# Fifteen of sixteen DMA engines for a weight load on the software queue, in place of fourteen

## The chip, the core and the metric

The kernel runs on one core of a Trainium2 chip. The metric is the device time in microseconds of one execution. A single profiled execution gives the durations below; the time before is the median of three other runs.

## The reference, cut to what matters

```python
# r_inputs [1024, 32, 128] float32, W [496, 128, 128] float32
I_IDX, J_IDX = the 496 pairs i < j of the 32 fields
transformed = einsum('bpd,ped->bpe', r_inputs[:, I_IDX, :], W)
y = transformed * r_inputs[:, J_IDX, :]          # [1024, 496, 128] float32, 260 MB
```

For each pair (i, j) of fields, field i is multiplied by the pair's own 128x128 matrix, and the product elementwise by field j. The matrices are 32.5 MB, the result 260 MB.

## The kernel before

The host lays the inputs out by field, transposed: a field is a tile of 128 partitions by 1024 columns (the batch). Pairs run from the last field backwards (`_pairs`), and each pair `q` has two halves of 512 columns. The first 15 pairs are multiplied in float32 directly (L267). For the other 481, weights and fields are split into a high part, a low part and a correction (`split_w`, L146 to L158; `split_x`, L163 to L177), and a half is three matmuls: two at L270 in `first`, a scaling of the PSUM tile on ScalarE at L272, and one at L281 in `second`, three halves later. VectorE multiplies the finished pair by field j into an output tile (`write`, L246), and ScalarE's queue stores the tile (L321): four pairs a store at first, three from pair 292 on (`FOURS`). Output tiles are a ring of 12 slots, and for a time the memory of fields that are loaded only later.

The program order is written out by hand in the loop at L302. What each step of it does to the DMA queues matters here:

- Stores go over ScalarE's queue, 128 rows each, so each of the 16 DMA engines carries eight rows of each store.
- Fields, and weights of chunks `c` that aren't in `WAPART`, are loaded over SyncE's queue (`load_x`, `load_group`, `load_w`), again eight rows to an engine. A chunk is the weights of eight pairs: a tile of 128 rows of 4 KB. Three tiles take turns (`WB`), and a chunk is loaded when the tile of an earlier one is spent (L327 to L335).
- The 25 chunks in `WAPART` (even `c` from 12 to 60) are loaded by `load_apart` (L113): the first `8 n` rows by one DMA of GpSimd, the software queue, whose source is arranged so that it falls into `n` shares of eight rows, one to an engine; the remaining rows by a DMA of SyncE, one or two to each engine. `n` is 14 for 17 of them and 12 for the other eight (every third, L35).
- The software queue hands its shares to consecutive engines, from where the last DMA ended. `move_on(k)` (L109) is a tiny DMA of `k` shares of two 64-byte rows into a scratch tile; it moves that place by `k`. `START` puts it at engine 5 once (L310). Each load of `n` shares is followed, three pairs later (`BACK`, L315 to L317), by `move_on(16 - n)`, which brings it round to 5. So a load of 14 shares is on engines 5 to 15, 0, 1 and 2, and skips 3 and 4; one of 12 shares skips 1 to 4. Engines are numbered here from the queue's first place.

Of the kernel before, what the change touches and what calls it, by code (L numbers as in the profile page):

```python
# [31 lines left out]

XG = 4
START = 5
WAPART = {c: 12 if k % 3 == 1 else 14 for k, c in enumerate(range(12, 62, 2))}  # L35
WLAST = max(WAPART)
BACK = 3
FOURS = 73
# [19 lines left out]
def kernel(  # L58
# [22 lines left out]
    nc = tc.nc  # L81
# [12 lines left out]
    def load_x(f, pieces=1, eng=None):  # L94
        if f == 0:

            t = rpool.tile([P, WL, P], F32, tag="w", name="x_0").rearrange("p q e -> p (q e)")
        else:
            t = xpool.tile([P, BT], F32, tag=f"x{f}", name=f"x_{f}")
        s = BT // pieces  # L100
        for k in range(pieces):
            (eng or nc.sync).dma_start(out=t[:, k * s : (k + 1) * s], in_=xt[f, :, k * s : (k + 1) * s])
        x_sb[f] = t

    w_raw = {}
# [3 lines left out]
    def move_on(k):  # L109

        nc.gpsimd.dma_start(out=mark[: 2 * k], in_=xt[0, : 2 * k, :16].rearrange("(b a) n -> a b n", a=k))

    def load_apart(c):  # L113
        n = WAPART[c]
        r = 8 * n
        nc.gpsimd.dma_start(out=w_raw[c][:r], in_=wt[c, :r].rearrange("(b a) m n -> a b m n", a=n))
        nc.sync.dma_start(out=w_raw[c][r:], in_=wt[c, r:])

    group = {}

    def load_group(k, m):
        if m == XG - 1:
            group[k] = xpool.tile([P, XG, BT], F32, tag=f"g{k}", name=f"x_g{k}")
        f = XG * k + 1 + m
        x_sb[f] = group[k][:, m, :]
        nc.sync.dma_start(out=x_sb[f], in_=xt[f])

    def load_w(c, splits=(0, WL), eng=nc.sync):
        w_raw[c] = rpool.tile([P, WL, P], F32, tag="w", name=f"w_{c}")
        if c in WAPART:  # L130
            load_apart(c)
            return
        for a, b in zip(splits, splits[1:]):
            eng.dma_start(out=w_raw[c][:, a:b, :], in_=wt[c, :, a:b, :])
# [78 lines left out]
    back = {}  # L213
# [45 lines left out]
    def first(u):  # L259
        q, h = divmod(u, 2)  # L260
        i, c = pairs[q][0], q // WC
        r = slice(q % WC * P, (q % WC + 1) * P)
        s = slice(h * HB, (h + 1) * HB)
        if h == 0:
            po[q] = po_t[q % PB]
        if q < nq0:
            nc.tensor.matmul(po[q][:, s], w_raw[q // WL][:, q % WL, :], x_sb[i][:, s], start=True, stop=True)  # L267
        else:
            for t in (0, 1):
                m = nc.tensor.matmul(po[q][:, s], w_s[c][t][:, r], x_s[i][t][:, s], start=t == 0, stop=t == 1)  # L270
                apart(m, scaled.get(u - 1) if h else None)
            scaled[u] = nc.scalar.mul(po[q][:, s], po[q][:, s], 1.0 + EPS)  # L272
            apart(scaled[u], taken.get(q - PB), "TensorE's products, which this waits for, have waited for it")

    def second(u):
        q, h = divmod(u, 2)
        i, j = pairs[q]
        r = slice(q % WC * P, (q % WC + 1) * P)
        s = slice(h * HB, (h + 1) * HB)
        if q >= nq0:  # L280
            m = nc.tensor.matmul(  # L281
                po[q][:, s], w_s[q // WC][2][:, r], x_s[i][2][:, s], start=False, stop=True, skip_group_check=True
            )
            apart(m, scaled[u ^ 1])
        g, k = group_of[q]
        if k == 0 and h == 0:
            ots[g] = out_tile(g)
        if q >= NQ - 2:
            write(g, k, s, po[q][:, s], x_sb[j][:, s])
        elif h == 1:  # L290
            taken[q] = write(g, k, slice(0, BT), po.pop(q), x_sb[j])
        ot = ots[g][0]
        n = groups[g][1]
        if q >= NQ - 2:
            stores.append((u + SLAG, rows(g)[:, k, s], ot[:, k, s]))
        elif g in (0, len(groups) - 1):
            if h == 1:
                stores.append((u + SLAG, rows(g)[:, k], ot[:, k]))
        elif k == n - 1 and h == 1:
            stores.append((u + SLAG, rows(g), ot))  # L300

    for u in range(2 * NQ + LAG + SLAG):  # L302
        q = u // 2
        if u < 2 * NQ:
            i, j = pairs[q]
            if u % 2 == 0 and j == i + 1 and XG * ngroup < i - 2 - XLEAD:
                load_x(i - 2 - XLEAD)
            first(u)
            if u == 2 * nq0:
                move_on(START)  # L310
            if u % 2 == 0 and q in group_at:
                load_group(*group_at[q])
            if u % 2 == 1 and q in w_at:
                load_w(w_at[q])
            if u % 2 == 0 and q in back:  # L315
                c = back.pop(q)
                move_on(16 - WAPART[c] if c < WLAST else 32 - START - WAPART[c])  # L317
        if LAG <= u < 2 * NQ + LAG:
            second(u - LAG)
        while stores and stores[0][0] <= u - LAG:  # L320
            nc.scalar.dma_start(*stores.pop(0)[1:])  # L321
        if u % 2 == 1:
            ready = [t for t in todo if t[0] <= q]
            if ready:
                ready[0][2](u)
                todo.remove(ready[0])
        if ring[WB:] and ring[0] in spent:  # L327
            ring.pop(0)
            c = ring[WB - 1]
            if c == "x":  # L330
                load_x(0)
            else:
                load_w(c)
            if c in WAPART:
                back[q + BACK] = c  # L335
        while later and later[0][0] <= u:
            nc.vector.tensor_tensor(*later.pop(0)[1:], ALU.subtract)  # L337
# [32 lines left out]
```

## Time and profile before

| | |
|---|---|
| median of three runs | 747.86 us (742.39 to 754.28) |
| the profiled execution's own time | 740.79 us |
| its span, first to last instruction | 738.9 us |
| HBM read, written | 49.29 MB, 260.05 MB; 419 GB/s over the span |
| mean granted TensorE clock | 0.990 |
| issue of a software-queue weight load | 17 of 448 KB, 8 of 384 KB; 0.62 us of GpSimd each |

The span is what the profile covers; the execution's own time is 1.9 us longer. The busy share of an engine is an average over stages; which engine sets the pace is read from the waits. A DMA's time to landing runs from its issue to the last of its 16 completion counts, so it holds the time in which the 16 engines work off what was queued before. The DMA share of a stretch is the time of all packets over 16 times its length.

### The profile page before, as it was taken

How to read it: one execution, taken by the hardware profiler on the slowest of the kernel's cores; microseconds unless marked ns; L12 is line 12 of the kernel's file. 1: busy time of each engine (PE TensorE's matmuls, PEld its weight loads, DVE VectorE, ACT ScalarE, POOL GpSimd, SP SyncE). 2: the span in 40 equal slices, each digit the busy share in tenths (PEclk: the TensorE clock that was granted, in tenths of full speed). 3: DMA queues.
4: the chain of work that ended last, by engine and by line, in shares of the span. 5: the costliest groups of instructions: out<-in, count | busy, mean ns of one | idle time of the engine just before them, and what ended most of it. 6: DMA issues, size and time to landing. Idle time of an engine off the chain costs nothing.

```text
span 738.9 us, 10346 instructions
## 1 busy us (share of the span) xinstructions
PE 702.5 (95%) x2946; PEld 548.9 (74%) x2946; DVE 636.5 (86%) x550; ACT 634.2 (86%) x1256; POOL 596.4 (81%) x882
## 2 busy tenths in 40 slices
PE   7999999999999999999899979999999999999993
PEld 3577777777878888787688858876887777877882
DVE  3888999999999998997789868977998888998894
ACT  1288989999999999998899969988999999998992
POOL 1789999999999999888879867987798878896660
PEclk9999999999999999999999989999999999999997
DMA  9999999999999999999999999999999999999998
GB/s 347 418 430 428 428 427 429 427 423 426 427 419 425 424 421 424 422 424 425 425 425 424 424 425 417 418 420 422 420 425 422 420 423 420 424 417 424 422 430 339
DMA packets 37096, 310.02 MB, mean 420 GB/s; under 512 B 5680, under 2 KB 5808, under 8 KB 19248
## 3 DMA queue, kind: packets, MB, share of 16 engines
q10 hardware_dynamic: 21888, 261.11, 83.8%
q1 hardware_dynamic: 10720, 37.30, 12.5%
q0 software_dynamic: 4432, 10.96, 3.8%
q8 instruction: 24, 0.39, 0.2%
q14 instruction: 32, 0.26, 0.1%
HBM read 49.29 MB, written 260.05 MB: 419 GB/s over the span
## 4 chain that ended last, share of the span: by engine, by line
PE 65%; DMA 19%; DVE 7%; POOL 3%; issue 2%; ACT 2%; SPq 0%; ACTq 0%; POOLq 0%; DVEq 0%
PE po L270 42%; PE po L281 20%; DMA out_dram<-slots 18%; DVE slots L246 4%; PE po L267 3%; DVE xd L337 2%; ACT po L272 2%; POOL wd L155 1%; POOL wl L153 1%; DMA x<-in_xt_dram 1%; POOL xl L170 1%; DVE ot L246 1%; POOL xl L171 0%; POOL wd L154 0%; ACT wh L151 0%
## 5 line engine op out<-in xcount | busy, mean ns | idle before, releaser
L272 ACT ACTIVATE po<-po 128x512 f32<-128x512 f32 x962 | 553.3, 584 | 72.5 <-PE po L270 55.1
L270 PE MATMUL po<-xh,wh 128*128 128x512 f32 x962 | 381.8, 397 | 16.8 <-DVE slots L246 13.5
L281 PE MATMUL po<-xd,wd 128*128 128x512 f32 x962 | 375.8, 391 | 4.8 <-DVE xd L337 2.4
L270 PE MATMUL po<-xl,wl 128*128 128x512 f32 x962 | 376.9, 392 | 1.3 <-POOL wl L153 1.0
L246 DVE TENSOR_TENSOR slots<-po,x 128x1024 f32<-128x1024 f32 (+1 forms) x263 | 313.7, 1213 | 53.0 <-DMA out_dram<-slots 18.7
L270 PEld LDWEIGHTS po<-xh,wh 128*128 128x128 f32 x962 | 181.0, 188 | 74.6 <-DVE slots L246 30.8
L153 POOL TENSOR_TENSOR wl<-w,wh 128x256 fp32r<-128x256 f32 x241 | 185.6, 770 | 61.7 <-ACT wh L151 55.6
L281 PEld LDWEIGHTS po<-xd,wd 128*128 128x128 f32 x962 | 180.9, 188 | 45.0 <-DVE slots L246 3.2
L270 PEld LDWEIGHTS po<-xl,wl 128*128 128x128 f32 x962 | 181.1, 188 | 40.8 <-POOL wl L153 4.0
L155 POOL TENSOR_TENSOR wd<-wl,wd 128x256 fp32r<-128x256 f32 x241 | 182.3, 757 | 20.1
L246 DVE TENSOR_TENSOR slots<-po,x_g 128x1024 f32<-128x1024 f32 x123 | 147.8, 1223 | 25.1 <-DMA out_dram<-slots 12.8
L246 DVE TENSOR_TENSOR ot<-po,x 128x1024 f32<-128x1024 f32 x99 | 119.3, 1221 | 14.0 <-PE po L281 4.9
L154 POOL TENSOR_SCALAR wd<-wh 128x256 fp32r<-128x256 f32 x241 | 102.6, 426 | 20.6
L151 ACT ACTIVATE wh<-w 128x256 fp32r<-128x256 f32 x241 | 98.7, 410 | 5.7 <-DVE slots L246 3.8
L337 DVE TENSOR_TENSOR xd<-xh,xl 128x512 fp32r<-128x512 f32 x52 | 48.1, 925 | 0.0
L170 POOL TENSOR_TENSOR xl<-x_g,xh 128x512 fp32r<-128x512 f32 x32 | 41.7, 1302 | 1.4 <-ACT xh L169 1.1
L170 POOL TENSOR_TENSOR xl<-x,xh 128x512 fp32r<-128x512 f32 x20 | 25.8, 1292 | 15.8 <-ACT xh L169 15.6
L171 POOL TENSOR_SCALAR xl<-xl 128x512 fp32r<-128x512 f32 x52 | 34.2, 658 | 4.6
L267 PE MATMUL po<-x,w 128*128 128x512 f32 x60 | 28.1, 625 | 4.3 <-DMA x<-in_xt_dram 4.3
L267 PEld LDWEIGHTS po<-x,w 128*128 128x128 f32 x60 | 11.6, 198 | 20.0 <-issue 13.7
L169 ACT ACTIVATE xh<-x 128x512 fp32r<-128x512 f32 x20 | 12.3, 624 | 11.5 <-DMA x<-in_xt_dram 11.4
L169 ACT ACTIVATE xh<-x_g 128x512 fp32r<-128x512 f32 x32 | 20.0, 624 | 0.0
(8 smaller groups left out, 49.9 us busy)
## 6 DMA issues: line engine op xcount, KB each, us to landing
out_dram<-slots ACTq DMA_DIRECT2D x67, 1536.0 KB, 12.7
out_dram<-slots ACTq DMA_DIRECT2D x44, 2048.0 KB, 16.4
out_dram<-ot ACTq DMA_DIRECT2D x28, 2048.0 KB, 13.8
w<-in_wt_dram SPq DMA_DIRECT2D x36, 512.0 KB, 10.9
x_g<-in_xt_dram SPq DMA_DIRECT2D x16, 512.0 KB, 16.3
w<-in_wt_dram POOLq DMA_DIRECT2D x17, 448.0 KB, 11.7
x<-in_xt_dram SPq DMA_DIRECT2D x14, 512.0 KB, 9.5
w<-in_wt_dram POOLq DMA_DIRECT2D x8, 384.0 KB, 12.0
```

Source lines behind the costliest of these rows:

```text
L151: halved[c] = nc.scalar.mul(h, raw, 1.0 - 2.0**-13)
L153: nc.gpsimd.tensor_tensor(l, raw, h.bitcast(F32), ALU.subtract)
L154: nc.gpsimd.tensor_scalar(d, h.bitcast(F32), EPS, 1.0, ALU.mult, ALU.mult)
L155: nc.gpsimd.tensor_tensor(d, l.bitcast(F32), d.bitcast(F32), ALU.subtract)
L170: nc.gpsimd.tensor_tensor(l, x_sb[f][:, s], h.bitcast(F32), ALU.subtract)
L171: nc.gpsimd.tensor_scalar(l, l.bitcast(F32), 1.0 / EPS, 1.0, ALU.mult, ALU.mult)
L246: i = nc.vector.tensor_tensor(ot[:, k, s], p, f, ALU.mult)
L267: nc.tensor.matmul(po[q][:, s], w_raw[q // WL][:, q % WL, :], x_sb[i][:, s], start=True, stop=True)
L270: m = nc.tensor.matmul(po[q][:, s], w_s[c][t][:, r], x_s[i][t][:, s], start=t == 0, stop=t == 1)
L272: scaled[u] = nc.scalar.mul(po[q][:, s], po[q][:, s], 1.0 + EPS)
L281: m = nc.tensor.matmul(po[q][:, s], w_s[q // WC][2][:, r], x_s[i][2][:, s], start=False, stop=True, skip_group_check=True)
L337: nc.vector.tensor_tensor(*later.pop(0)[1:], ALU.subtract)
```

## The change

Seventeen of the 25 chunks get `n = 15` in place of 14, so that only engine 4 is skipped; the eight with 12 shares stay as they are. The last eight rows of the seventeen leave SyncE's queue: a second DMA of GpSimd (`rest`) loads them, one row to each of eight consecutive engines, at the place in the program where the place of the queue is brought round. It comes before a `move_on(9)` for chunks with `c % 4 == 2` and behind it for chunks with `c % 4 == 0`, so that the eight rows are on engines 4 to 11 or on 13 to 15 and 0 to 4: 15 + 8 + 9 = 32 shares either way. The last chunk is followed by `move_on(4)`. SyncE issues 17 DMAs less, GpSimd 17 more (887 instructions become 904); the order on the other engines doesn't change.

```diff
-WAPART = {c: 12 if k % 3 == 1 else 14 for k, c in enumerate(range(12, 62, 2))}
+WAPART = {c: 12 if k % 3 == 1 else 15 for k, c in enumerate(range(12, 62, 2))}
...
         nc.gpsimd.dma_start(out=w_raw[c][:r], in_=wt[c, :r].rearrange("(b a) m n -> a b m n", a=n))
-        nc.sync.dma_start(out=w_raw[c][r:], in_=wt[c, r:])
+        if n == 12:
+            nc.sync.dma_start(out=w_raw[c][r:], in_=wt[c, r:])
+
+    def go_round(c):
+
+        def rest():
+            a, b = [t[120:].rearrange("a (b m) n -> a b m n", b=2) for t in (w_raw[c], wt[c])]
+            nc.gpsimd.dma_start(out=a, in_=b)
+
+        if WAPART[c] == 12:
+            move_on(4)
+        elif c == WLAST:
+            rest()
+            move_on(4)
+        elif c % 4:
+            rest()
+            move_on(9)
+        else:
+            move_on(9)
+            rest()
...
-                c = back.pop(q)
-                move_on(16 - WAPART[c] if c < WLAST else 32 - START - WAPART[c])
+                go_round(back.pop(q))
```

## The prediction

> **What bounds the kernel now.** I read the page first (busy shares, slices, DMA queues), then the windows by stage, then the waits, the chain, and the DMA issues.
>
> ```profile
> span 738.9 us, 10346 instructions
> PE 702.5 (95%) x2946; PEld 548.9 (74%) x2946; DVE 636.5 (86%) x550; ACT 634.2 (86%) x1256; POOL 596.4 (81%) x882
> DMA  9999999999999999999999999999999999999998
> q10 hardware_dynamic: 21888, 261.11, 83.8%
> q1 hardware_dynamic: 10720, 37.30, 12.5%
> q0 software_dynamic: 4432, 10.96, 3.8%
> ```
>
> The DMA queues add up to 100.4% of 16 engines' span: q10 (the stores, from ACT) 83.8, q1 (loads from SP) 12.5, q0 (the software queue) 3.8. No DMA engine ever rests.
>
> ```profile
> 20.00:125.00 105.00, 100.76 (x404) 74.73 (x402) 97.02 (x85) 85.12 (x172) 93.31 (x128) 1.00 1.01 428
> 125.00:320.00 195.00, 192.95 (x833) 154.90 (x834) 179.41 (x156) 182.11 (x364) 177.66 (x261) 1.00 1.01 424
> 320.00:690.00 370.00, 355.84 (x1521) 283.22 (x1520) 316.12 (x274) 329.87 (x653) 300.08 (x453) 0.99 1.01 422
> 690.00:735.00 45.00, 37.23 (x161) 29.65 (x159) 35.05 (x31) 33.16 (x65) 21.37 (x34) 0.96 1.00 421
> ```
>
> By stage (stretch, its length, then PE, PEld, DVE, ACT, POOL busy, granted clock, DMA share, GB/s) the DMA share is 1.0 everywhere, and PE is at 96 to 99% until 690 us. Two bounds lie close together; a DMA engine that gets later shows up as a late store:
>
> ```profile
> POOL wl L153 <- ACT wh L151: 55.6, 65, 7.8
> DVE slots L246 <- DMA out_dram<-slots: 31.6, 40, 6.4
> PEld po L270 <- DVE slots L246: 30.8, 44, 5.9
> PEld po L270 <- POOL wl L153: 4.0, 8, 1.2
> PE po L270 <- POOL wl L153: 1.0, 2, 0.8
> ```
>
> (who waits for whom: total us, times, longest). DVE waits 31.6 us for stores to leave their slots, and PE then waits for DVE. PE waits for POOL only 5.0 us in all.
>
> ```profile
> out_dram<-slots ACTq DMA_DIRECT2D x67, 1536.0 KB, 12.7
> w<-in_wt_dram POOLq DMA_DIRECT2D x17, 448.0 KB, 11.7
> w<-in_wt_dram SPq DMA_DIRECT2D x18, 64.0 KB, 6.1
> mark<-in_xt_dram POOLq DMA_DIRECT2D x16, 0.2 KB, 9.5
> L111 POOL DMA_DIRECT2D mark<-in_xt_dram x26: 634/634/748, 31.5 to 679.6; - x26
> L117 SPq DMA_DIRECT2D w<-in_wt_dram x25: 326/326/338, 124.5 to 675.2; - x25
> ```
>
> A store is done when the last of its engines is done, and so is the kernel. The question is therefore which engine is last, and by how much.
>
> **The engines one by one.** A packet in the trace has queue, start, duration and size, and no engine. But each starts 3 or 4 ns before the end of the one ahead of it on its engine, so I strung them, from the end backwards, into 16 chains, each holding its share of every load and store in order. This holds from 331 us on. The software rows name the chains: a 14-share load with the cursor at 5 falls on engines 5 to 15, 0, 1, 2; a 12-share one on 5 to 15 and 0. Last packets end: engines 1 and 2 at 737.5 and 737.0, 0 at 737.0, one of 5 to 15 at 737.3, the others at 734.5 to 735.9; engines 3 and 4, in an order that I can't tell, at 735.6 and 734.0.
>
> Before, the 25 loads give engines 0 and 5 to 15 17x9 + 8x10 = 233 rows each, 1 and 2 169, and 3 and 4 33. So 3 and 4 have 200 rows less, at 155 ns from start to start (a 4 KB packet takes 159) 31 us less work, and still end with the others: their packets are that much slower. Over the medians (611 ns for 16 KB, 460 for 12, 159 for 4) the packets from 345 us on lose: 3 and 4 21.7 and 18.8 us, 1 and 2 7.4 and 8.2, 0 4.2, the other eleven 0.5 to 3.6.
>
> The losses are of two kinds. One of {3, 4} loses 8.8 of its 21.7 us in steps up to 50 ns on nearly every packet, also after 695 us when no load moves: 1.3 us in 700 to 735. Call it the steady one. The other loses 16.7 of its 18.8 us in bursts of 2 to 3 us while a weight load moves, 0.5 to 0.7 us a load; engines 1 and 2 lose in the same bursts. In the bursts, lead matters: 1 and 2 lose 0.6 to 1.2 us in SP loads that find them 0.5 us ahead to 1.3 behind the median, and mostly nothing from 1.8 us behind on. Before 125 us, where no load skips an engine, the stores' landings show one engine drifting behind (3.1 us behind the median at 120 us), a few settling about 1.4 behind, and all packets together lose 1 to 2 us in 20, against 4 to 5 later. So the bursts look like the price of being ahead, and the steady loss belongs to one engine.
>
> **The change, part by part.**
> (1) Rows: in 17 loads 15 shares skip only engine 4, and the last eight rows go one to an engine, nine times to 4 to 11, eight times to 13 to 15 and 0 to 4. Engine 3 has 17x8 + 8 + 16 = 160 rows, +127, or 127 x 0.155 = +19.7 us; engine 4 stays at 33; 0, 1, 2, 13, 14, 15 lose 9 rows (-1.4 us), 5 to 11 8 (-1.2), 12 17 (-2.6).
> (2) Small packets: engine 3 drops 17x8 four-byte dummies (9 ns each, 5 to 6 from start to start), -0.7 us; each new DMA adds about three small ones an engine, 17 x 15 ns = 0.3 us. Together about 0.
> (3) SP issues 17 DMAs less (17 x 0.33 = 5.5 us); SP does nothing else near then: 0.
> (4) POOL issues 17 more: 17 x 0.634 = 10.7 us, in order with its splits of w and x. POOL is idle 142 us; PE waits for it 5.0 us in all. 0 taken; 10.7 if all of it lay on the path; a gain is excluded, as POOL loses nothing.
> (5) Later landing: the last rows were issued by SP 1.23 us ahead of the POOL load; now 2.7 to 4.8 us behind it, plus 0.64 where the mark goes first. With a mark's longest landing, 12.6 us, that is 18 us after the load at worst; the first split of such a tile comes 19.3 to 26.4 us after it (the one tile used after 11.4 us is a 12-share one, which stays). The ACT split would wait for it, with the scalings queued behind; hidden by at least 1 us. Nor does a mark wait for more: the semaphores that it shares are eight DMAs old, now some 70 us instead of 90.
> A rule that speaks against parts 4 and 5 stands in the Trainium skill, "DMA: Bandwidth & Descriptors", "Rules for kernel authors": small transfers should be merged, since below 64 KB one pays mostly overhead. By that page's fit (2.0 us and the bytes, "Anatomy of one DMA") 17 transfers of 32 KB would cost 17 x 2.1 = 36 us, an estimate, if each stood on the path; the trace's 64 KB loads landed in 6.1 us beside engines that never rest, so the time is latency and not work.
>
> So only engine 3 can cost. Its cost is bounded from above by no relief, and from below by full relief, after which engines 1 and 2, 9 rows lighter, set the end: -1.4 us. If engine 3 is the burst one, it then has the rows and the place of engines 1 and 2, which carry just this and end at 737.3. I take that end: the burst losses of 1 and 2 depend on lead, and those before 125 us nearly vanish. That 4 is the steady one I take from nothing but the nesting of skips; the trace can't say.
>
> Sum: profiled execution 740.79 us (span 738.9) - 1.4 = 739.4. The median of the three runs shown is 747.86, 0.95% above the profiled one; on that scale 747.86 - 1.4 = 746.4.
>
> **Rivals.**
> B, slower: engine 3 is the steady one. It loses 3.1 to 3.5 us in 100 (3.1 at 120 us; 1.3 in 37 at the end), 22 to 25 us in 710, and only the 64 rows by which it is below the others (9.9 us) make up for it: 12 to 15 behind a median of 735 - 1.2, so 746 to 749 against 737.5, +8 to +11.5 us with no bursts on it, up to C's +17.4 with all of them. I take +11.5, 759 on the runs' scale. For: it is one of two, and the trace doesn't name them. It decides by which of the two drifts.
> C, slower: the bursts hit engine 3 whatever its lead. 19.7 - 0.4 from 734.0 or 735.6 gives 753.3 to 754.9 against 737.5: +15.8 to +17.4, 764 to 765. For: its burst loss is 0.5 to 0.7 us at leads from 2 us ahead to none. Against: engines 1 and 2, and the stage before 125 us.
> D: POOL becomes the bound, at most +10.7 us, 757. Against: 142 us of idle time.
> E, faster by over 2%: every loss over the medians vanishes. From 20 us on they are 126 us on 16 engines, 7.9 each; not 15.
>
> **How the numbers follow.** Chances: forecast 0.55, B 0.22, C 0.18, D 0.03, E 0.02. The forecast's own range is 742 to 752 (-1.4 to +2 us, and the scatter of the runs, 742 to 754). The whole range reaches over B and C: 740 to 765. A change of about 2% (15 us) is what a measurement of this kernel can tell from none. B lies at +1.1 to +2.3% and C at +2.1 to +2.3%: a third of the one (0.07) and most of the other (0.13) count as slower, and 0.02 for scatter: slower 0.22. Faster 0.03, for E and scatter; the rest is same, 0.75.
>
> **What would show it.** In the profile after: the same DMA share of 1.0; 4 KB packets moved from SP's queue to the software queue, 17x16 = 272 of them; the last stores' landing spread still 3 to 4 us. If engine 3 is late, the spread of a store's 16 landings grows through the run towards 8 us and more, the 1536 KB stores take 15 us or more to land instead of 12.7, and DVE's 31.6 us of waiting for stores rises by as much as the span. If POOL is to blame, PE's 5.0 us behind POOL rise. What would make the forecast wrong is a loss on engine 3 that goes on once it has fallen 2 us behind.

## The result, and the profile after

The changed kernel takes 750.19 us, the median of 20 runs (749.80 to 751.07). The kernel before takes 746.79 us, the median of 20 runs (742.39 to 754.28). The ratio is 1.0061, with a 95% interval of 1.0042 to 1.0080: 0.6% slower. Ratios, here and below, leave out runs more than 1.5% above the fastest of their kernel and are not the quotients of the medians, which here is 1.0046. The forecast was 746.4 us, a gain of 1.4; the time lies inside the range of 740 to 765, on the other side of the kernel before.

The profiled execution takes 749.80 us (span 748.0), against 740.79 before (738.9). That is +9.0 us. Most of the gap between 9.0 and 3.4 is the execution that the profile of before happened to catch, one of the quickest of its kernel: the runs of before scatter over 12 us, those after lie within 1.3.

The page of the changed kernel: span, engines, the DMA share in 40 slices, GB/s in 40 slices, and the queues.

```profile
span 748.0 us, 10339 instructions
...
PE 705.9 (94%) x2946; PEld 549.0 (73%) x2946; DVE 635.2 (85%) x550; ACT 635.2 (85%) x1256; POOL 604.9 (81%) x899
...
DMA  9999999999999999999999998999999999999997
GB/s 344 424 429 428 422 419 426 426 421 418 415 420 422 422 429 422 427 420 428 421 425 423 427 407 338 420 423 425 422 422 420 417 421 420 423 412 418 418 425 288
...
q10 hardware_dynamic: 21888, 261.11, 82.8%
q1 hardware_dynamic: 10176, 36.18, 12.2%
q0 software_dynamic: 4976, 12.09, 4.3%
```

q1 has 544 packets and 1.1 MB less, q0 as much more: 17 DMAs of 16 rows of 4 KB (272 packets), and as many small packets. The three queues now fill 99.3% of 16 engines' span, where they filled 100.1% before (100.4% in the prediction, which counts two small queues with them). Slice 25 of the GB/s row has 338 where before had 417: engines have begun to rest. The windows around a pause in which TensorE's clock is granted by half for 6.8 us show it best. First the kernel before, then after (stretch, its length, PE, PEld, DVE, ACT and POOL busy, clock, DMA share, GB/s):

```profile
300.00:434.00 134.00, 130.17 (x560) 103.70 (x559) 115.64 (x102) 122.26 (x243) 112.77 (x168) 1.00 1.01 424
434.00:446.00 12.00, 6.49 (x21) 4.92 (x20) 5.41 (x6) 4.20 (x10) 4.00 (x7) 0.72 1.01 429
```

```profile
300.00:440.00 140.00, 134.10 (x570) 105.47 (x570) 118.99 (x104) 124.45 (x245) 117.03 (x178) 1.00 1.01 424
440.00:452.00 12.00, 6.28 (x21) 4.74 (x20) 5.04 (x5) 4.24 (x9) 4.35 (x7) 0.72 0.78 329
```

In both kernels the clock is 0.72 over these 12 us and less is produced. Before, the engines had enough queued to work through it (share 1.01). After, the share is 0.78: engines had worked off their queues, while one was still busy with old stores, as the landings below show.

The waits of the changed kernel (who waits for whom: total us, times, longest):

```profile
PEld po L289 <- DVE slots L265: 37.5, 53, 6.1
DVE slots L265 <- DMA out_dram<-slots: 31.3, 37, 6.6
PE po L289 <- DVE slots L265: 18.0, 21, 5.7
...
PEld po L289 <- POOL wl L172: 6.0, 10, 1.2
...
PE po L289 <- POOL wl L172: 2.3, 4, 0.7
```

TensorE's waits for VectorE to empty PSUM into slots have grown: from 30.8 to 37.5 us for the weight loads (PEld) and from 13.5 to 18.0 for the matmuls (PE). This is the row of PE before:

```profile
PE po L270 <- DVE slots L246: 13.5, 16, 5.5
```

Weight loads overlap matmuls, so the two rows can't be added up to lost time: PE stands idle 42.1 us in all (748.0 less 705.9), 36.4 before, while the span has grown by 9.1. The two rows behind POOL sum to 8.3 us, 5.0 before. Two signs that the prediction named for a late engine did not come: DVE's direct wait for stores has not grown (31.3, 31.6 before), and the 1536 KB stores land after 12.8 us, not 15 (12.7 before). By what path the late stores reach TensorE is not settled: on the chain of work that ended last, DMAs take 28% after, 19% before and 30% in e3 below, but 20% in e7, which takes as long as the changed kernel. The sign that did come is the spread of the landings.

Every store leaves 16 completion counts, one by each engine. Read off the trace, mean over the stores issued in a stretch, the last of the 16 comes behind their median by (us; in brackets the last but one):

| stores issued at | 20-80 | 140-200 | 260-320 | 320-380 | 380-440 | 440-500 | 620-680 |
|---|---|---|---|---|---|---|---|
| before | 1.4 (1.1) | 2.1 (1.4) | 1.8 (1.0) | 1.7 (1.5) | 1.0 (0.9) | 1.3 (0.8) | 2.3 (2.1) |
| after | 1.2 (0.9) | 2.8 (1.6) | 4.7 (2.7) | 6.3 (3.0) | 6.9 (3.2) | 2.9 (1.4) | 5.1 (2.4) |

After the first loads of the change one engine pulls away from the others, is 6.9 us late before the pause, makes up 4 us in it while others rest, and falls behind again.

The first software-queue load after the pause shows that it isn't engine 4. The load is issued at 454.6 us with 15 shares. Its first completion comes after 1.7 us, behind a run of small packets 5 to 8 ns apart, too close for a store's packet (460 to 611 ns) between them: that is the engine without a share, engine 4, and it had nothing else queued. The next completion comes after 5.0 us and the last after 9.2. So the late engine has a share of the load, and of the 15 that have one only engine 3 has more rows than before.

Stores are issued 0.8 us later than before at 149 us, 3.0 at 288, 6.5 at 433 and 8.5 at 676.

### The profile page after: what moved, and what is told of

It reads as the page before. It is cut to its first block, busy times and chain, and to the rows that moved or that the text cites. A ratio compares the mean times of both kernels' runs of the same rounds, so it can differ in the third digit from the quotient of the medians.

```text
span 748.0 us, 10339 instructions
## 1 busy us (share of the span) xinstructions
PE 705.9 (94%) x2946; PEld 549.0 (73%) x2946; DVE 635.2 (85%) x550; ACT 635.2 (85%) x1256; POOL 604.9 (81%) x899
## 4 chain that ended last, share of the span: by engine, by line
PE 54%; DMA 28%; DVE 9%; POOL 5%; issue 2%; ACT 0%; ACTq 0%; DVEq 0%; POOLq 0%
PE po L289 34%; DMA out_dram<-slots 23%; PE po L300 17%; DVE slots L265 6%; DMA out_dram<-ot 4%; PE po L286 4%; DVE xd L355 2%; DVE ot L265 1%; POOL wl L172 1%; POOL wd L174 1%; POOL xl L189 1%; POOL wd L173 1%; DMA x<-in_xt_dram 1%; POOL xl L190 0%; ACT po L291 0%
## 5 line engine op out<-in xcount | busy, mean ns | idle before, releaser
L265 DVE TENSOR_TENSOR slots<-po,x 128x1024 f32<-128x1024 f32 (+1 forms) x263 | 313.8, 1213 | 58.5 <-DMA out_dram<-slots 18.8
L289 PEld LDWEIGHTS po<-xh,wh 128*128 128x128 f32 x962 | 181.0, 188 | 80.1 <-DVE slots L265 37.5
L174 POOL TENSOR_TENSOR wd<-wl,wd 128x256 fp32r<-128x256 f32 x241 | 180.2, 748 | 20.1
L355 DVE TENSOR_TENSOR xd<-xh,xl 128x512 fp32r<-128x512 f32 x52 | 46.6, 896 | 0.0
## 6 DMA issues: line engine op xcount, KB each, us to landing
out_dram<-slots ACTq DMA_DIRECT2D x67, 1536.0 KB, 12.8
```

What stands on the lines that cost most here:

```text
L174: nc.gpsimd.tensor_tensor(d, l.bitcast(F32), d.bitcast(F32), ALU.subtract)
L265: i = nc.vector.tensor_tensor(ot[:, k, s], p, f, ALU.mult)
```

## The experiments

The theory after the result (1): the late engine is engine 3, and its added rows set the end. The rivals (2): the 17 DMAs more that GpSimd issues (2a), or the later landing of the last rows (2b). Ratios are to the kernel before, on the same chip, with 95% intervals; its medians there were 746.2 to 747.5 us.

**e1_more_marks.** The kernel before; at six go-rounds one mark of 2 shares becomes four of 34 together, two rounds of the 16 engines more, so that the place comes out the same.

```diff
-                move_on(16 - WAPART[c] if c < WLAST else 32 - START - WAPART[c])
+                if c in (16, 28, 36, 40, 48, 52):
+                    for k in (13, 4, 15, 2):
+                        move_on(k)
+                else:
+                    move_on(16 - WAPART[c] if c < WLAST else 32 - START - WAPART[c])
```

> The kernel before, with the one mark of two shares behind six of the 14-share loads replaced by four marks of 13, 4, 15 and 2 shares: GpSimd issues 18 DMAs more, no row changes its engine, nothing lands later. The marks also tell engine 3 from engine 4 in the trace. If the rows on engine 3 cost the time: same as before, ratio 1.000 (0.997 to 1.003). If GpSimd's 17 more issues cost it: 1.004 to 1.008, as after the change.

Measured: 807.72 us, ratio 1.0833 (1.0793 to 1.0874). Both expectations miss, and its waits say why:

```profile
PEld po L270 <- POOL wl L153: 80.2, 13, 15.6
POOL mark L111 <- DMA mark<-in_xt_dram: 79.9, 18, 9.9
...
PE po L270 <- POOL wl L153: 74.9, 6, 15.2
```

All marks write the same scratch tile, so each of the 18 added ones waited for the landing of the one ahead of it, 79.9 us in all, with GpSimd's splits queued behind. It is no test of issues alone; it shows what a wait on GpSimd costs when it is not hidden.

**e2_rows_on_pool.** The kernel before, but the last 16 rows of the 17 loads go on the software queue ahead of the go-round, one row to each of 16 engines. No engine has more or fewer rows than before.

```diff
-        nc.sync.dma_start(out=w_raw[c][r:], in_=wt[c, r:])
+        if n == 12:
+            nc.sync.dma_start(out=w_raw[c][r:], in_=wt[c, r:])
...
                 c = back.pop(q)
+                if WAPART[c] == 14:
+                    a, b = [t[112:].rearrange("a (b m) n -> a b m n", b=2) for t in (w_raw[c], wt[c])]
+                    nc.gpsimd.dma_start(out=a, in_=b)
```

> The kernel before, with the last 16 rows of the seventeen 14-share loads moved from SyncE's queue to the software queue, one to each engine, three pairs later: every engine keeps its rows. GpSimd issues 17 DMAs more and the rows land later. If the rows on engine 3 cost the time: 1.000 (0.997 to 1.003). If the issues, or the later landing, cost it: 1.004 to 1.008.

Measured: 748.84 us (743.51 to 755.72), ratio 1.0044 (1.0012 to 1.0075). By itself that spoke for 2a or 2b; e5, e6 and e11 below take it back.

**e3_skip_three.** The mirror of the change: the loads of 15 shares skip engine 3, and engine 4 takes the rows. By the places of the queue it has 165 rows, 132 more than before and five more (0.8 us) than engine 3 in the change; the 127 and 160 in the expectations are a little short.

```diff
-START = 5
+START = 4
...
         if WAPART[c] == 12:
-            move_on(4)
+            move_on(3)
         elif c == WLAST:
             rest()
-            move_on(4)
-        elif c % 4:
-            rest()
-            move_on(9)
+            move_on(5)
         else:
-            move_on(9)
-            rest()
+            k = 9 if WAPART[c + 2] == 15 else 10
+            if c % 4:
+                rest()
+                move_on(k)
+            else:
+                move_on(k)
+                rest()
```

> The changed kernel, with the fifteen shares on all engines but 3 in place of all but 4; the 12-share loads still skip 1 to 4. Engine 4 takes the 127 rows. If the two engines are alike: the same as the change, 1.006 (1.003 to 1.009). If one of them loses time steadily and it is engine 4: slower, 1.010 to 1.020, with one engine's last writes 8 us or more behind the median. If it is engine 3: faster than the change, 0.996 to 1.002.

Measured: 760.96 us (760.58 to 761.11), ratio 1.0210 (1.0173 to 1.0247), 10.8 us above the change. Which engine takes the rows matters, with as many issues and rows that land as late; the five rows more account for 0.8 of the 10.8 us. The last landing of a store is 9.8 us behind the median before the pause (the last but one 1.9), and in the pause engines run empty (share 0.75):

```profile
440.00:460.00 20.00, 14.01 (x50) 10.71 (x49) 10.56 (x10) 10.99 (x22) 9.78 (x16) 0.83 0.75 312
```

**e4_half_the_dose.** Nine of the seventeen loads as in the change, eight as before.

```diff
-WAPART = {c: 12 if k % 3 == 1 else 15 for k, c in enumerate(range(12, 62, 2))}
+WAPART = {c: 12 if k % 3 == 1 else 15 if c % 4 or c == 60 else 14 for k, c in enumerate(range(12, 62, 2))}
```

> Nine of the seventeen loads with 15 shares as in the change, eight with 14 shares as before: engine 3 has 72 + 16 = 88 to 100 rows, between the 33 and the 160. If the rows on engine 3 cost the time in proportion: 1.003 (1.001 to 1.005). If engine 3 takes up some rows for nothing, as losses that depend on its lead would let it: 1.000 or less (0.995 to 1.001).

Measured: 744.13 us (743.17 to 750.37), ratio 0.9997 (0.9966 to 1.0027). Half of the rows cost nothing.

**e5_issues_alone.** The kernel before with 17 tiny DMAs more on the software queue, into a tile of their own.

```diff
+    mark2 = xpool.tile([32, 16], F32, tag="mark2", name="mark2")
+    def once_round():
+        nc.gpsimd.dma_start(out=mark2, in_=xt[0, :32, :16].rearrange("(b a) n -> a b n", a=16))
...
                 c = back.pop(q)
+                if WAPART[c] == 14:
+                    once_round()
```

> The kernel before with seventeen more small DMAs on the software queue, two 64-byte rows to each of its 16 engines, into a tile of their own, each ahead of a go-round of a 14-share load: POOL's 17 issues of 0.63 us without any weight row moved. Theory 1 (the end is set by engine 3's added rows, the issues are hidden): 746 us, ratio 0.997 to 1.003. Theory 2a (the issues on POOL cost): as the kernel with the last 16 rows on that queue, ratio 1.004, 749 us, and up to +10.7 us if each lies on the path; PE's waits for POOL above 5.0 us. Theory 2b (the late landing of the last rows costs): 746 us.

Measured: 743.32 us (739.44 to 748.99), ratio 0.9954 (0.9923 to 0.9984). The waits of PE for POOL's split are close to those of the changed kernel, 8.0 us (8.3 there), and the profiled span is 737.6, below that of before:

```profile
PEld po L275 <- POOL wl L158: 5.8, 9, 1.2
...
PE po L275 <- POOL wl L158: 2.2, 4, 0.7
```

So 17 issues go with 3 us more of waits for POOL, and the end does not come later. 2a falls.

**e6_rows_at_once.** As e2, with the 16 rows issued right behind the load.

```diff
-        nc.sync.dma_start(out=w_raw[c][r:], in_=wt[c, r:])
+        if n == 12:
+            nc.sync.dma_start(out=w_raw[c][r:], in_=wt[c, r:])
+        else:
+            a, b = [t[112:].rearrange("a (b m) n -> a b m n", b=2) for t in (w_raw[c], wt[c])]
+            nc.gpsimd.dma_start(out=a, in_=b)
```

> The kernel before with the last 16 rows of the seventeen loads on the software queue, issued right behind the load and not three pairs later. Theory 1: 746 us, ratio 0.997 to 1.003, as every engine has its rows of before. Theory 2a (issues on POOL): ratio 1.004, 749 us, as with the rows issued later. Theory 2b (late landing): 746 us, the +0.4% of the later rows gone.

Measured: 746.83 us (742.09 to 755.90), ratio 1.0002 (0.9966 to 1.0037). Again no cost of the issues, nor of having 272 more rows on the software queue, as many as the change moves there.

**e7_all_at_once.** The changed kernel with the last eight rows and the go-round issued right behind the load.

```diff
             load_apart(c)
+            if WAPART[c] == 15:
+                go_round(c)
             return
...
-                go_round(back.pop(q))
+                c = back.pop(q)
+                if WAPART[c] == 12:
+                    go_round(c)
```

> The changed kernel with the last eight rows and the go-round of the seventeen loads issued right behind the load: the same DMAs on the same engines in the same order, three pairs earlier. Theory 1 (engine 3's rows): 750 us, ratio 1.004 to 1.008, as tight as the changed kernel. Theory 2a (issues on POOL): 750 us too. Theory 2b (late landing): 747 us, ratio 1.001.

Measured: 750.40 us, ratio 1.0036 (1.0007 to 1.0065), eleven of its twelve runs between 749.89 and 751.32, as the changed kernel. Landing the last rows earlier wins nothing back: 2b falls for the change.

**e8_thirteen_loads.** Thirteen of the seventeen loads as in the change.

```diff
-WAPART = {c: 12 if k % 3 == 1 else 15 for k, c in enumerate(range(12, 62, 2))}
+WAPART = {c: 12 if k % 3 == 1 else 14 if c in (18, 30, 42, 54) else 15 for k, c in enumerate(range(12, 62, 2))}
```

> The changed kernel with 13 of its 17 loads over 15 engines and four over 14 as before. Engine 3 has 30 to 31 rows less than in the changed kernel, 4.7 us of its own work. Theory 1: with engine 3 ending at 746.5 - 4.7 = 741.8 us in the trace, level with the others at 742, so 745 to 747, ratio 0.998 to 1.001, between the nine loads (744.1) and the seventeen (750.2), and the landings of a store 2 to 4 us apart instead of 6.9. Theory 2 (a cost for each issue or late row): 13/17 of +3.4 us, 749 us, ratio 1.0035 to 1.0045.

Measured: 746.64 us (745.59 to 759.40), ratio 0.9998 (0.9970 to 1.0026): between the nine loads and the seventeen, as theory 1 has it. The last landing is 7.0 us behind the median before the pause and 4.0 at 620 to 680 us, where 2 to 4 were expected. Engine 3 has 28 rows less than in the change, not 30 to 31: the four loads' last 16 rows put one on it again.

By rows on engine 3 the medians are: 33 rows 746 to 747 us, 96 (e4) 744.1, 132 (e8) 746.6, 160 (the change) 750.2. The last 28 rows are 4.3 us of transfer at 0.155 us each and cost 3.6. The first 63 rows cost nothing, so up to there engine 3 does not set the end.

**e9_no_software_queue.** All 25 loads whole on SyncE's queue. The host still lays out their rows for the shares, so the rows of these matrices arrive in another order and the products are others; bytes and work are the same.

```diff
-        nc.gpsimd.dma_start(out=mark[: 2 * k], in_=xt[0, : 2 * k, :16].rearrange("(b a) n -> a b n", a=k))
+        pass
...
-        n = WAPART[c]
-        r = 8 * n
-        nc.gpsimd.dma_start(out=w_raw[c][:r], in_=wt[c, :r].rearrange("(b a) m n -> a b m n", a=n))
-        nc.sync.dma_start(out=w_raw[c][r:], in_=wt[c, r:])
+        nc.sync.dma_start(out=w_raw[c], in_=wt[c])
```

> The kernel before with all 25 weight loads whole on SP, 200 rows to each of the 16 engines, and no software queue: no marks, no issue on POOL. In the kernel that skips engine 3, engine 4 with 160 rows lost 38.0 us over the nominal durations in 736 us and ended at 757.9. Theory A (the loss belongs to the engine, whatever queue the loads go through and however late it is): 40 rows more, +6.2 us, so engine 4 ends at 764, 766 to 768 us, ratio 1.025 to 1.03, with landings 9 us and more apart. Theory B (the part above the 2.7 to 3.1 us per 100 us seen before 125 us comes with the software queue's loads): engine 4 loses 23 us and ends near 749, 751 us, ratio 1.003 to 1.008.

Measured: 754.11 us (753.42 to 754.28), ratio 1.0118 (1.0094 to 1.0142). Between the two, nearer to B. One engine falls 8.9 us behind before the pause. With 200 rows on every engine, 35 more than on engine 4 in e3, it ends 7 us earlier than e3.

**e10_nine_and_rounds, e11_before_again, e12_rounds_everywhere.** e10 is e4 with the tiny DMA of e5 at the eight go-rounds of 14-share loads; e12 has it at all seventeen; e11 is the kernel before, unchanged.

> Nine of the seventeen loads over 15 engines as in the half dose, and a small 16-engine DMA ahead of the go-round of the eight others. If the 0.46% of the kernel with seventeen such DMAs is real and adds to the half dose, ratio 0.992 to 0.996, 741 to 743 us; if it was scatter, as the half dose, 744 us, 0.997 to 1.003.

> The kernel before, unchanged, as one more kernel of the comparison: what the measurement itself makes of no change. If its 95% interval is to be trusted, the ratio lies within 0.997 to 1.003. A ratio of 0.995 or 1.004 here would mean that the effects of that size in the kernels with more DMAs on the software queue are scatter.

> As the kernel of nine loads over 15 engines with a small 16-engine DMA at eight go-rounds, but with that DMA at all seventeen. If those DMAs themselves make the kernel faster, by about 0.27% for eight of them and 0.46% for seventeen, ratio 0.990 to 0.993, 739 to 740 us. If they do nothing and the ratios 0.9954 and 0.9942 were scatter about the half dose, 0.994 to 1.000, 741 to 744 us. If POOL's issues begin to cost, above 744 us.

Measured: e10 741.46 us (740.64 to 746.55), ratio 0.9942 (0.9911 to 0.9973); e11 746.83, ratio 1.0030 (1.0002 to 1.0059); e12 743.30 (741.49 to 747.77), ratio 0.9975 (0.9946 to 1.0004). The unchanged kernel comes out at 1.003, with 1 just outside its interval. So 0.3 to 0.5% in either direction can't be told from nothing here, and e2's +0.44% and e5's -0.46% can't be called effects of their DMAs. The change's own 0.6% is not far above that band either; what carries it is not the ratio alone but the tight repeats of the change and of e7, and e3, 2.1% slower by the same means. More of the tiny DMAs (e12) are not faster than fewer (e10). The three kernels with nine loads of 15 shares have medians of 741.5, 743.3 and 744.1, ratios 0.994 to 1.000: e10 had the fastest median of all, and half of the change is no loss and perhaps a gain of some 0.3%; more the runs don't carry.

The time of the changed kernel, on the other hand, repeats within 0.2% in 20 runs and in eleven of e7's twelve (the other took 755.44 us). That tightness fits the finding: with one engine late, its own work sets the end.

## Why the prediction was wrong

**Right.** The rows (part 1) and the packets moved came out as worked out. The small packets, SP's issues and POOL's issues cost nothing that shows: e5, e6. The later landing is hidden: e7. Engine 4, not 3, is the worse of the two, a step that the prediction took "from nothing but the nesting of skips": e3 is 10.8 us above the change.

**The step that failed** is the relief: "the burst losses of 1 and 2 depend on lead, and those before 125 us nearly vanish", so that engine 3, once behind, would lose next to nothing and leave engines 1 and 2 to set the end, at -1.4 us. For that it had to win back 17.2 to 18.8 us of losses: without relief it would end at 753.3 to 754.9 (rival C), and the forecast has the end at 737.5 - 1.4 = 736.1. It ended at 746.5, so by this profile of before it won back 6.8 to 8.4. How much it loses when late can be measured in the traces of kernels with one late engine, since the last of a store's 16 landings is then that engine's. Its work between two such landings is its packets at the medians that the prediction used, less 3.5 ns each for the overlap from start to start; what is left of the time is its loss, to about 1 us (a rest counts too, but a late engine has work queued).

| engine, kernel | stretch, us | work | loss | per 100 us |
|---|---|---|---|---|
| 3, after | 22.3 to 746.9 | 697.1 | 27.4 | 3.8 |
| 3, after, 3 to 7 us late | 243.9 to 341.2 | 92.1 | 5.2 | 5.3 |
| 3, after, 5 to 8 us late | 346.5 to 439.9 | 88.6 | 4.9 | 5.2 |
| 3, after, to the end | 346.5 to 746.9 | 384.3 | 16.1 | 4.0 |
| 4, e3 | 22.1 to 757.9 | 697.7 | 38.0 | 5.2 |
| 4, e3, to the end | 351.5 to 757.9 | 384.8 | 21.7 | 5.3 |
| the late one, e9 | 22.8 to 751.3 | 702.9 | 25.6 | 3.5 |

The prediction's two chains lost 21.7 and 18.8 us from 345 us on. Engine 4, 9 us late in e3, lost 21.7 in about as long: no relief at all. Engine 3, late in the change, lost 16.1 against the 18.8 of its chain (the other chain being engine 4's, as e3 makes likely): 2.7 us of relief, not 18.8. At its latest it lost 5.2 to 5.3 us per 100, more than its average. So an engine that is late goes on losing; being behind does not end it. What engines 1 and 2 showed, on which the step was read, was lead and loss side by side; that the one caused the other was argued, not shown. Nor do these losses explain themselves: why an engine loses them is open, but for the part that goes with the software queue (below).

**The size.** Rival C had the mechanism and too high a price: of the 6.8 to 8.4 us that it is over, 2.7 are the relief after 345 us. The rest falls before 345 us, where the packets of before could not be strung to engines; whether engine 3 rested there or lost less afterwards stays open. Rival B came nearer to the end in the trace (a loss of 3.1 to 3.5 us in 100 on engine 3, an end at 746 to 749 us; measured 3.8 in 100 and 746.5), but by luck, since it made engine 3 the worse of the two, and its 759 us on the runs' scale were not measured.

**The base.** The sum was made against a profile that ended at 737.5. A second trace of the same kernel, e11's, has a span of 744.2, and from 200 us on the last landing of its stores is 3.5 to 4.8 us behind the median and the last but one 3.0 to 4.7, where the profile shown has 0.8 to 2.5 for the last. In such a run two engines are late without the change, and they are neither 3 nor 4: in the load issued at 451.6 us, just after the pause, the two engines without a share have their completions first, after 1.8 and 2.1 us with only small packets to do, the next comes after 5.0, and the last two, from engines with a share, after 9.2 and 9.5. Against such a run engine 3's 746.5 is 3.7 us behind the last packet (742.8 us), and the change costs 0.6% and not 1.2%. The prediction scaled the whole profile by 0.95% as if the scatter were spread over everything. What makes engines of before late in some runs and not in others stays open.

## What to carry to other kernels

Where every DMA engine is busy all the time, work on the engines one by one: give a slow engine less, raise its share in steps, and look for the step at which the last of a store's landings leaves the others. In this kernel 63 rows below that step were free, and the last 28 above it cost 3.6 of their 4.3 us. An engine's losses under load should be taken as its own until a run with that engine late shows otherwise; and one profile of a kernel whose runs scatter by 1.6% is not a base for a forecast of 0.2%.

## What the runs showed of the hardware

- The two engines are not slow in the same measure, 27.4 and 38.0 us in some 730, and part of it goes with the software queue. Without that queue (e9) the latest engine, whichever it is, lost 25.6 us, so engine 4 lost at least 12 us less than in e3, where it was 38.0. The Trainium skill, "DMA: Bandwidth & Descriptors", section "Latency and other measured facts", says that two of the engines are usually slower than the rest, guesses that traffic for the descriptors of the software queue is the reason, and says that this is particular to that queue. The runs agree as to two slow engines and as to a part that goes with the queue; they show that a loss of 3.5 us per 100 on one engine stays without it, and they cannot name the engines by the page's numbers.
- With one engine late, the runs of a kernel agree within 1.3 us (the change, 20 runs; e3 0.5 us, e9 0.9 us; e7 but for one of twelve runs); those of the kernel before scatter by 12 us.
- The pause of TensorE at half clock, which cost the DMA engines nothing before (share 1.01), is where a late engine catches up (6.9 to 2.9 us) while others idle (0.78).
- GpSimd's DMAs into one scratch tile, issued one behind the other, each waited for the landing of the one ahead: 18 waits, 79.9 us, up to 9.9 each, and +8% of time (e1). Seventeen into a tile of their own, far apart, cost nothing that shows (e5).
